# Two chained cross-attentions in float32: heads moved to ACT, a longer lead of the query products, an earlier turned weight, and the last subtile placed among the output products

## The chip, the core and the metric

The kernel runs on one core of one Trainium2 chip. The metric is the device time of one execution in microseconds (us); the median of three runs before the change is 1940.47 us. The engines are called PE (TensorE, with PEld for its weight loads), DVE (VectorE), ACT (ScalarE), POOL (GpSimd) and SP (SyncE, which here only issues DMA transfers). ACT and POOL issue DMA transfers too.

## The reference

There are B=4 sequences of L=1024 tokens with width H=1024, all float32, and a context of S=64 tokens per sequence. Two cross-attention layers follow each other.

```python
# layer 0: 32 query heads of 32, 8 key/value heads
q = x @ Wq + bq;  k = ctx @ Wk + bk;  v = ctx @ Wv + bv
scores = q k^T / sqrt(32) + mask[b, 1, L, S]
out = (softmax(scores) @ v) @ Wo + bo
x = layernorm(out + x) * gamma + beta
# layer 1: 16 heads of 64
a = layernorm(ctx) * ln_gamma + ln_beta
Q = x @ Wq1^T;  K = a @ Wk1^T;  V = a @ Wv1^T
scores = Q K^T / 8, masked keys set to -inf
x = x + tanh(gate) * (softmax(scores) @ V) @ Wo1^T
```

## The kernel before

**Tiles.** The 4096 tokens are 32 subtiles of 128, four blocks of 8 subtiles (`SUB`, `NBLK`; a block is one sequence), or 16 pairs of subtiles. Large products use a seven-product scheme in the manner of Strassen: of a weight and of the token block, quarters and sums of quarters are kept (`B11`, `T1`, `S2`, `N4` and so on), and seven products of half size give what eight would.

**Layer-0 queries.** `query_steps` (L559) is a list of 28 products for a block. Each is four matmul instructions with 512 columns (the trace counts eight) into one of four single PSUM banks (`wx`). `keep` (L576) lets ACT copy a bank to SBUF with the bias, `add` (L582) lets DVE add another bank to that copy, and `put` (L579) stores the result to `qTd` in DRAM over SP's queue. `load_queries` (L636) fetches a subtile's queries from there. The four copies per block are named e, z, u and f; e, u and f share three buffers, z has two.

**Layer-0 attention.** `mix(t, count)` works on subtile t and calls, between its steps, `count` items of a generator `other_work`. The steps of a subtile have two halves of 16 heads: `front` (scores, L669, and mask add, L673), `largest` (maximum, L680, and its subtraction, L683), exponentials on ACT, `total` (sum, L700, reciprocal, L701), `divide` (L704). Of a subtile up to 18 (`by_turning`), the 16 heads of half 0 are exponentiated on ACT one by one (`some`, L687), with the negative maximum as bias and the sum accumulated, so that L683 and L700 are left out for them. The other half is one ACT instruction (`others`, L695). The probabilities are turned through DRAM for these subtiles: `p` is stored (L717) and read back as quarters `pq` (L721), both on POOL's queue, and DVE turns blocks of 32x32 (`turn_quarters`, L405). From subtile 19 on, PE transposes them (`turn`, L396) and ACT copies them (L400). Then come `values` (L740), a copy `oT` by ACT (L389) and its store `oTd` on ACT's queue (L746). The tile `s` of a subtile has two buffers, two-bank PSUM tiles (`big`) are two.

**The other work.** `other_work` (L906) gives the query products of blocks 1 to 3 and then, for each of 8 chunks k of the layer-1 query weight wq1, the folding of the layer-1 keys into that weight (`folded_queries`, L836): one item in which PE turns the chunk (L396) and ACT copies it (L387), and four items `heads` (L850, copied by ACT at L856); the results `a` are stored to `ad` (L862). Within it the quarters of w_o are loaded at the start, their four sums (L181 to L184) are made after chunk 3, and the first pair's tiles `o` and `r` are loaded after chunk 5. `AHEAD = 4` items run before subtile 0; the other 80 are spread evenly over subtiles 0 to 23; eight fold items follow, and the other 32 over subtiles 24 to 31. So the first queries of a block are loaded after the last of its 28 products.

**After attention.** The last subtile (31) is turned and multiplied, the pools of attention are closed, new ones are opened, and `left_out` makes the four differences of the first pair. Then a loop over 16 pairs does the output products (`project`, L421: seven products, L429, gathered by DVE, L437) with a list `fill` of small steps between them: `folded_values` (L877, L882) for the first 8 pairs, and the layer norm of the pair before. Layer 1 follows with the same kind of products on the folded weights.

**Order.** The program is traced in the order of the Python code, and a scheduler then reorders instructions on each engine by estimated costs, with DMA issues on the queue of the engine that issues them. `keep_in_program_order` pins an instruction behind all that were traced before it on its engine. Engines start instructions in that order. Semaphores join the engines.

**The first block.** Before attention starts, the loop over `query_steps(0, ...)` runs the first 28 products; a dictionary `fills` gives the steps after which the next block's rows are turned by DVE. Ahead of this the layer-0 keys and values are stored to `kTd` and `vTd` (L814).

Of the kernel before, what the change touches and what calls it, by code (L numbers as in the profile page):

```python
# [14 lines left out]
P = 128  # L15
H = 1024
# [18 lines left out]
BY_HEAD = 16  # L35
# [36 lines left out]
def tile_two_cross_attentions(  # L72
# [56 lines left out]
    bd = dram.tile([B, H, H], F32, tag="bd", name="bd")  # L129

# [55 lines left out]

    def right_weight(w, tag, name, turned=False):

        r = {"B11": block_of(w, 0, 0, tag, f"{name}_B11", turned)}
        r["T1"] = block_of(w, 0, 1, tag, f"{name}_B12", turned)  # L190
        r["B22"] = block_of(w, 1, 1, tag, f"{name}_B22", turned)
        r["B21"] = block_of(w, 1, 0, tag, f"{name}_B21", turned)
        for n in ("T3", "T2", "N4"):
            r[n] = new_block(tag, f"{name}_{n}")
        return r, right_sums(r)
# [195 lines left out]
    def turn(nat, dst, singles=False):  # L391

        ps = [wx(), wx()] if singles else big()
        for k in range(KC):
            at = ps[k // HK][:, sub_ap(k % HK)] if singles else ps[:, sub_ap(k)]
            nc.tensor.transpose(at, nat[:, sub_ap(k)], ident)  # L396
        if singles:
            copy_out(dst.rearrange("p k l -> p (k l)"), ps)
        else:
            nc.scalar.copy(dst, ps.rearrange("p (k l) -> p k l", k=KC))  # L400

    def turn_quarters(t, dst, ks):

        k0, k1 = ks
        nc.vector.transpose(  # L405
            dst.rearrange("p k (u i) -> p k u i", i=Q),
            t[:, :, k0 * Q : k1 * Q].rearrange("p u (k j) -> p k u j", j=Q),
        )
# [234 lines left out]
    def attend0(t):  # L643
# [12 lines left out]

        n = BY_HEAD if by_turning(t) else 0

# [20 lines left out]
        def largest(e):  # L679
            nc.vector.tensor_reduce(mx[:, e], heads[:, e], AX.XY, ALU.max, negate=True)  # L680
            k = slice(0 if e else n, 16)
# [15 lines left out]
        def total(e):  # L697
            k = slice(0 if e else n, 16)
# [7 lines left out]
        exps = [lambda lo=lo: some(lo, min(lo + 4, n)) for lo in range(0, n, 4)]  # L706
        exps = exps[:1] + [lambda: others(1)] + exps[1:] if n else [lambda: others(0), lambda: others(1)]
# [114 lines left out]

    early_cm.close()
# [12 lines left out]
    def folded_queries(kT, wch, k):  # L836

        wT = wpool.tile([P, KC, P], F32, tag="wb", name=f"wq1T_{k}")
        st = [wpool.tile([P, B, 512], F32, tag="wb", name=f"a_{k}_{n}") for n in range(2)]

        def first():
            turn(wch, wT, True)
# [23 lines left out]
        return [first] + [lambda cc=cc: heads(cc) for cc in range(4)]  # L866
# [26 lines left out]
    def load_outputs(pair):  # L893
        o = (o2pool if pair else early).tile([P, KC, 2 * P], F32, tag="o2", name=f"o2_{pair}")
        nc.sync.dma_start(out=o, in_=oTd[pair])
        r = []
        for u in range(2):
# [3 lines left out]
            nc.sync.dma_start(out=ru, in_=x[sub_ap(t), :])  # L901
# [4 lines left out]
    def other_work(rows):  # L906
# [20 lines left out]
        wch = chunk(wq1, 0, "wq1")  # L927
        w_o, w_o_sums = right_weight(wo0, "wa", "wo0", "heads")
        bo_sb = constant(bo0.partition_broadcast(P), [P, H], "bo", F32, fold)
        for k in range(KC):  # L930
            ahead = chunk(wq1, k + 1, "wq1") if k + 1 < KC else None
            for step in folded_queries(kT, wch, k):
                step()
                yield
            wch = ahead
            if k == 3:
                run(w_o_sums)
            if k == 5:
                first_outputs = load_outputs(0)
# [4 lines left out]
    AHEAD = 4  # L944
# [269 lines left out]
```

## Time and profile before

| | us |
|---|---|
| runs | 1940.96, 1937.8, 1940.47 |
| median | 1940.47 |
| the profiled execution's own time | 1938.62 |
| its span, from first to last instruction | 1936.8 |
| PE busy | 1880.2 |
| DVE busy | 1307.3 |
| ACT busy | 384.6 |
| front of subtile 0 starts | 193.84 |
| front of subtile 20 starts | 529.30 |
| front of subtile 24 starts | 605.23 |
| last subtile's transposes start | 714.59 |

A sum of changes is made against 1938.62; what lies outside its span is 1.82 us, and the median is 1.85 us above it. The last four rows are read from the timeline of PE; they cut the kernel into the stages that the text below speaks of. "Busy" counts an engine's instructions without DMA issues and waits; an instruction's row in the groups has its mean duration in nanoseconds, and the idle time ahead of it with what ended most of it. A wait "X <- Y" in the list of waits names the instruction that waited and the one that released it; the numbers are total us, times, longest us. The row PEclk, and the granted clock in a window, are TensorE's clock as a share of full speed.

### The profile page before, as it was taken

How to read it: one execution, taken by the hardware profiler on the slowest of the kernel's cores; microseconds unless marked ns; L12 is line 12 of the kernel's file. 1: busy time of each engine (PE TensorE's matmuls, PEld its weight loads, DVE VectorE, ACT ScalarE, POOL GpSimd, SP SyncE). 2: the span in 40 equal slices, each digit the busy share in tenths (PEclk: the TensorE clock that was granted, in tenths of full speed). 3: DMA queues.
4: the chain of work that ended last, by engine and by line, in shares of the span. 5: the costliest groups of instructions: out<-in, count | busy, mean ns of one | idle time of the engine just before them, and what ended most of it. 6: DMA issues, size and time to landing. Idle time of an engine off the chain costs nothing.

```text
span 1936.8 us, 17075 instructions
## 1 busy us (share of the span) xinstructions
PE 1880.2 (97%) x6160; PEld 890.1 (46%) x6160; DVE 1307.3 (67%) x1572; ACT 384.6 (20%) x1028; POOL 135.8 (7%) x134
## 2 busy tenths in 40 slices
PE   8999999998998889999999999999999999999999
PEld 7744444444445654334344444444444444444444
DVE  3424799898878974566478777557665766576653
ACT  1111554553435761221200001000000000000000
POOL 0000111111100102111122200000000000000000
PEclk9999999999999889999999999999999999999999
DMA  8971689797768875666673344374747474747421
GB/s 281 184 187 65 171 243 269 231 258 232 232 184 249 266 257 184 218 208 191 215 208 119 130 110 122 99 180 125 179 127 177 128 176 130 174 131 173 120 87 43
DMA packets 218180, 342.10 MB, mean 177 GB/s; under 512 B 25456, under 2 KB 140528, under 8 KB 213104
## 3 DMA queue, kind: packets, MB, share of 16 engines
q1 hardware_dynamic: 156736, 255.03, 46.8%
q10 hardware_dynamic: 52544, 46.14, 8.6%
q0 software_dynamic: 8816, 39.85, 7.1%
q8 instruction: 48, 0.79, 0.2%
q14 instruction: 36, 0.29, 0.1%
HBM read 203.34 MB, written 137.63 MB: 176 GB/s over the span
## 4 chain that ended last, share of the span: by engine, by line
PE 80%; DVE 12%; DMA 3%; issue 3%; ACT 2%; POOL 0%; SPq 0%; DVEq 0%; ACTq 0%; POOLq 0%
PE wx L429 58%; PE wx L565 12%; PE big L669 2%; DVE mx L680 2%; DVE s L673 2%; PE wx L368 1%; PE big L368 1%; PE big L877 1%; DVE s L683 1%; DVE pT L405 1%; DMA q<-qTd 1%; DVE sm L700 1%; DVE s L704 1%; PE big L740 1%; ACT s L687 1%
## 5 line engine op out<-in xcount | busy, mean ns | idle before, releaser
L437 DVE TENSOR_TENSOR r<-wx,r 128x512 f32<-128x512 f32 x224 | 153.5, 686 | 236.3 <-PE wx L429 223.4
L491 ACT ACTIVATE s<-s 128x1024 f32<-128x1024 f32 x32 | 33.7, 1057 | 651.8 <-DVE s L490 651.8
L441 DVE TENSOR_TENSOR s<-wx,key_bias 128x512 f32<-128x512 f32 x64 | 44.1, 690 | 136.7 <-PE wx L429 136.7
L565 PE MATMUL wx<-xT,wq_S 128*128 128x512 f32 x256 | 119.0, 600 | 0.8 <-ACT z L576 0.8
L429 PE MATMUL wx<-wo_B,S 128*128 128x512 f32 x256 | 117.1, 600 | 1.9 <-DVE r L437 1.9
L902 POOL TENSOR_TENSOR r<-r,bo 128x1024 f32<-128x1024 f32 x32 | 82.1, 2571 | 491.9 <-DMA r<-in_x_dram 184.0
L429 PE MATMUL wx<-b_B,pT 128*128 128x512 f32 x256 | 115.8, 593 | 0.6 <-ACT pT L400 0.6
L565 PE MATMUL wx<-xB,wq_A 128*128 128x512 f32 x256 | 116.1, 598 | 0.0
L429 PE MATMUL wx<-b_B,S_p 128*128 128x512 f32 x256 | 116.0, 596 | 0.0
L429 PE MATMUL wx<-a_B,xT 128*128 128x512 f32 x256 | 115.4, 592 | 0.0
L429 PE MATMUL wx<-a_B,S_x 128*128 128x512 f32 x256 | 115.3, 593 | 0.1
L429 PE MATMUL wx<-wo_B,o 128*128 128x512 f32 x256 | 114.6, 595 | 0.0
L687 ACT ACTIVATE s<-s,mx 128x64 f32<-128x64 f32 x304 | 101.1, 335 | 55.4 <-DVE mx L680 49.3
L673 DVE TENSOR_TENSOR s<-big,m 128x1024 f32<-128x1024 f32 x64 | 77.2, 1219 | 38.2 <-PE big L669 38.1
L669 PE MATMUL big<-kv,q 64*128 64x128 f32 x1024 | 86.3, 301 | 9.5 <-DMA q<-qTd 9.3
L669 PEld LDWEIGHTS big<-kv,q 64*128 64x128 f32 x1024 | 74.6, 204 | 43.7 <-issue 36.7
L405 DVE STREAM_TRANSPOSE pT<-pq 128x1024 f32<-128x1024 f32 x66 | 77.9, 1219 | 1.8 <-DMA pq<-p 1.8
L429 PEld LDWEIGHTS wx<-wo_B,S 128*128 128x128 f32 x256 | 47.1, 190 | 68.6 <-issue 51.2
L704 DVE TENSOR_TENSOR s<-s,sm 128x1024 f32<-128x1024 f32 x64 | 76.8, 1219 | 0.9
L429 PEld LDWEIGHTS wx<-wo_B,o 128*128 128x128 f32 x256 | 48.0, 190 | 63.5 <-issue 61.9
L429 PEld LDWEIGHTS wx<-a_B,S_x 128*128 128x128 f32 x256 | 48.5, 190 | 62.0 <-issue 58.3
L429 PEld LDWEIGHTS wx<-a_B,xT 128*128 128x128 f32 x256 | 48.7, 190 | 61.2 <-issue 60.5
(158 smaller groups left out, 2916.4 us busy)
## 6 DMA issues: line engine op xcount, KB each, us to landing
p<-s POOLq DMA_DIRECT2D x19, 1024.0 KB, 7.6
pq<-p POOLq DMA_DIRECT2D x76, 256.0 KB, 5.8
xq<-in_x_dram SPq DMA_DIRECT2D x64, 256.0 KB, 10.0
q<-qTd SPq DMA_DIRECT2D x32, 512.0 KB, 7.6
oTd<-oT ACTq DMA_DIRECT2D x32, 512.0 KB, 6.8
ad<-a SPq DMA_DIRECT2D x16, 1024.0 KB, 6.4
o<-oTd SPq DMA_DIRECT2D x16, 1024.0 KB, 5.3
r<-in_x_dram SPq DMA_DIRECT2D x32, 512.0 KB, 5.5
```

The lines of the kernel that those rows point to most:

```text
L368: nc.tensor.matmul(ps[:, 0:256], w[k // HK, c // HK][:, k % HK, sub_ap(c % HK)], ct[:, k, :], start=(k == 0), stop=(k == KC - 1),)
L405: nc.vector.transpose(dst.rearrange("p k (u i) -> p k u i", i=Q), t[:, :, k0 * Q : k1 * Q].rearrange("p u (k j) -> p k u j", j=Q),)
L429: nc.tensor.matmul(bank, a[s][:, k, :], w[m][:, k, :], start=first and k == 0, stop=last and k == HK - 1, skip_group_check=True,)
L437: nc.vector.tensor_tensor(at, bank, at, ALU.add)
L441: nc.vector.tensor_tensor(at, bank.rearrange("p (h s) -> p h s", s=S), bias.unsqueeze(1).to_broadcast([P, 512 // S, S]), ALU.add,)
L565: nc.tensor.matmul(bank, w_q[a][:, k, sub_ap(i)], rows[b][:, k, :], start=first and k == 0, stop=last and k == HK - 1, skip_group_check=True,)
L669: nc.tensor.matmul(ps[:, at : at + P], q[on, c * 4 + g, :], k0bd[on, b, c, :], start=True, stop=True,)
L673: nc.vector.tensor_tensor(quarters[:, :, c * 8 : (c + 1) * 8], ps.rearrange("p (k a l) -> p a k l", a=NQ, l=Q), mask.rearrange("p e (h l) ...
L680: nc.vector.tensor_reduce(mx[:, e], heads[:, e], AX.XY, ALU.max, negate=True)
L687: nc.scalar.activation(heads[:, 0, k], heads[:, 0, k], AF.Exp, bias=mx[:, 0, k : k + 1], accum_out=sm[:, 0, k : k + 1],)
L704: nc.vector.tensor_tensor(heads[:, e], heads[:, e], wide(sm[:, e]), ALU.mult)
L902: nc.gpsimd.tensor_tensor(ru, ru, bo_sb, ALU.add)
```

## The change

1. `BY_HEAD` becomes a pair (16, 8): of half 1 too, eight heads of subtiles 0 to 18 are exponentiated one by one on ACT, 24 in all; L683 and L700 of that half cover eight heads in place of 16.
2. The layer-1 query weight is turned in the first block. A pool of two buffers of rows and two of columns takes each chunk of 128 rows with four loads on SP's queue; DVE turns it (`turn_quarters`, pinned in program order) after steps 6, 8, 10, 12, 14, 16, 19 and 21; four stores on POOL's queue write it to `wq1T` in DRAM. The folding later loads `turned_chunk(k)` from there. An item of PE transposes per chunk is gone, so that 32 fold items are left of 40.
3. `AHEAD` becomes 6. Blocks 1 and 2 are spread as 28 products over 8 subtiles each, so that the lead is still 6 when the next block begins; over subtiles 16 to 23 come the other 22. `FOLD_AHEAD = 6` fold items follow, and 26 over subtiles 24 to 31.
4. The loads of the quarters of w_o come after chunks 1 to 4 and their sums after chunk 5. `left_out` of the first pair is moved into `other_work`, its result in the pool `early`, and the first pair's loads are pinned.
5. The turning of subtile 31, its values, the closing and opening of pools and the loads of the second pair become the first entries of `fill`, between the first pair's output products.

```diff
@@ -32,7 +32,7 @@
 QW = H // NQ
 PPB = NPAIR // B
 HEADS0 = 32
-BY_HEAD = 16
+BY_HEAD = 16, 8
 
 
 
@@ -127,6 +127,7 @@
     vTd = dram.tile([P, KC, B * S], F32, tag="vTd", name="vTd")
     ad = dram.tile([B, H, H], F32, tag="ad", name="ad")
     bd = dram.tile([B, H, H], F32, tag="bd", name="bd")
+    wq1T = dram.tile([H, H], F32, tag="wq1T", name="wq1T")
 
     def open_pool(stack, name, bufs, side="left"):
         return stack.enter_context(tc.tile_pool(name=name, bufs=bufs, side=side, reuse_waits="tile"))
@@ -184,14 +185,23 @@
             lambda: tt(r["N4"], r["B21"], r["T2"], ALU.subtract),
         ]
 
+    def right_loads(w, tag, name, turned=False):
+
+        r = {}
+
+        def load(n, i, j):
+            r[n] = block_of(w, i, j, tag, f"{name}_B{i + 1}{j + 1}", turned)
+
+        def last():
+            load("B21", 1, 0)
+            for n in ("T3", "T2", "N4"):
+                r[n] = new_block(tag, f"{name}_{n}")
+
+        return r, [lambda: load("B11", 0, 0), lambda: load("T1", 0, 1), lambda: load("B22", 1, 1), last]
+
     def right_weight(w, tag, name, turned=False):
-
-        r = {"B11": block_of(w, 0, 0, tag, f"{name}_B11", turned)}
-        r["T1"] = block_of(w, 0, 1, tag, f"{name}_B12", turned)
-        r["B22"] = block_of(w, 1, 1, tag, f"{name}_B22", turned)
-        r["B21"] = block_of(w, 1, 0, tag, f"{name}_B21", turned)
-        for n in ("T3", "T2", "N4"):
-            r[n] = new_block(tag, f"{name}_{n}")
+        r, loads = right_loads(w, tag, name, turned)
+        run(loads)
         return r, right_sums(r)
 
     def run(steps):
...
@@ -654,7 +660,7 @@
         mx = small.tile([P, 2, 16], F32, tag="mx0", name=f"mx_0_{t}")
         sm = small.tile([P, 2, 16], F32, tag="sm0", name=f"sm_0_{t}")
 
-        n = BY_HEAD if by_turning(t) else 0
+        alone = BY_HEAD if by_turning(t) else (0, 0)
 
         def wide(v):
             return v.unsqueeze(2).unsqueeze(3).to_broadcast([P, v.shape[-1], 2, Q])
@@ -678,24 +684,24 @@
 
         def largest(e):
             nc.vector.tensor_reduce(mx[:, e], heads[:, e], AX.XY, ALU.max, negate=True)
-            k = slice(0 if e else n, 16)
+            k = slice(alone[e], 16)
             if k.start < 16:
                 nc.vector.tensor_tensor(heads[:, e, k], heads[:, e, k], wide(mx[:, e, k]), ALU.add)
 
-        def some(lo, hi):
+        def some(e, lo, hi):
             for k in range(lo, hi):
                 nc.scalar.activation(
-                    heads[:, 0, k], heads[:, 0, k], AF.Exp, bias=mx[:, 0, k : k + 1],
-                    accum_out=sm[:, 0, k : k + 1],
+                    heads[:, e, k], heads[:, e, k], AF.Exp, bias=mx[:, e, k : k + 1],
+                    accum_out=sm[:, e, k : k + 1],
                 )
 
         def others(e):
-            k = slice(0 if e else n, 16)
+            k = slice(alone[e], 16)
             if k.start < 16:
                 nc.scalar.activation(heads[:, e, k], heads[:, e, k], AF.Exp)
 
         def total(e):
-            k = slice(0 if e else n, 16)
+            k = slice(alone[e], 16)
             if k.start < 16:
                 nc.vector.tensor_reduce(sm[:, e, k], heads[:, e, k], AX.XY, ALU.add)
             nc.vector.reciprocal(sm[:, e], sm[:, e])
@@ -703,8 +709,13 @@
         def divide(e):
             nc.vector.tensor_tensor(heads[:, e], heads[:, e], wide(sm[:, e]), ALU.mult)
 
-        exps = [lambda lo=lo: some(lo, min(lo + 4, n)) for lo in range(0, n, 4)]
-        exps = exps[:1] + [lambda: others(1)] + exps[1:] if n else [lambda: others(0), lambda: others(1)]
+        if by_turning(t):
+            one_by_one = [
+                [lambda e=e, lo=lo: some(e, lo, lo + 4) for lo in range(0, alone[e], 4)] for e in range(2)
+            ]
+            exps = one_by_one[0][:1] + [lambda: others(1)] + one_by_one[1] + one_by_one[0][1:]
+        else:
+            exps = [lambda: others(0), lambda: others(1)]
         return front, largest, exps, total, divide
 
     def outputs0(t):
@@ -813,13 +824,36 @@
     for dst, kvT in kv1:
         nc.sync.dma_start(out=dst, in_=kvT)
     kv1_cm.close()
+    wq1_cm = ExitStack()
+    wq1pool = open_pool(wq1_cm, "wq1", 2, "right")
+
+    wq1_rows = {}
+
+    def load_wq1(n):
+        if n < KC:
+            wq1_rows[n] = wq1pool.tile([P, NQ, QW], F32, tag="rows", name=f"wq1_{n}")
+            load_quarters(wq1_rows[n], wq1[sub_ap(n), :])
+
+    def turn_wq1(n):
+
+        cols = wq1pool.tile([P, KC, P], F32, tag="cols", name=f"wq1c_{n}")
+        tc.keep_in_program_order(turn_quarters(wq1_rows.pop(n), cols, (0, KC)))
+        load_wq1(n + 2)
+        to = wq1T[:, sub_ap(n)].rearrange("(a k j) i -> a j k i", a=NQ, j=Q)
+        for a in range(NQ):
+            nc.gpsimd.dma_start(out=to[a], in_=cols[a * Q : (a + 1) * Q])
+
+    for n in range(2):
+        load_wq1(n)
     steps = query_steps(0, rows)
     rows, fills = rows0(1)
+    fills.update({n: lambda i=i: turn_wq1(i) for i, n in enumerate((6, 8, 10, 12, 14, 16, 19, 21))})
     for n, step in enumerate(steps):
         step()
         if n in fills:
             fills[n]()
 
+    wq1_cm.close()
     early_cm.close()
     qpool = open_pool(attention, "q0", 2, "right")
     spool = open_pool(attention, "scores", 2, "right")
@@ -833,13 +867,14 @@
         nc.sync.dma_start(out=t, in_=w[sub_ap(k), :])
         return t
 
-    def folded_queries(kT, wch, k):
-
-        wT = wpool.tile([P, KC, P], F32, tag="wb", name=f"wq1T_{k}")
+    def turned_chunk(k):
+        t = wpool.tile([P, KC, P], F32, tag="wb", name=f"wq1T_{k}")
+        nc.sync.dma_start(out=t, in_=wq1T[:, sub_ap(k)].rearrange("(c p) i -> p c i", p=P))
+        return t
+
+    def folded_queries(kT, wT, k):
+
         st = [wpool.tile([P, B, 512], F32, tag="wb", name=f"a_{k}_{n}") for n in range(2)]
-
-        def first():
-            turn(wch, wT, True)
 
         def heads(cc):
             banks = [wx(), wx()]
@@ -863,7 +898,7 @@
                     out=ad[:, sub_ap(k), n * 512 : (n + 1) * 512].rearrange("b p o -> p b o"), in_=st[n]
                 )
 
-        return [first] + [lambda cc=cc: heads(cc) for cc in range(4)]
+        return [lambda cc=cc: heads(cc) for cc in range(4)]
 
     def folded_values(vT, wch, c):
 
@@ -892,13 +927,17 @@
 
     def load_outputs(pair):
         o = (o2pool if pair else early).tile([P, KC, 2 * P], F32, tag="o2", name=f"o2_{pair}")
-        nc.sync.dma_start(out=o, in_=oTd[pair])
+        load = nc.sync.dma_start(out=o, in_=oTd[pair])
+        if not pair:
+            tc.keep_in_program_order(load)
         r = []
         for u in range(2):
             t = pair * 2 + u
             ru = (rpool.tile([P, H], F32, tag="r", name=f"r_{t}") if pair
                   else early.tile([P, H], F32, tag="r", name=f"r_{t}", bufs=2))
-            nc.sync.dma_start(out=ru, in_=x[sub_ap(t), :])
+            load = nc.sync.dma_start(out=ru, in_=x[sub_ap(t), :])
+            if not pair:
+                tc.keep_in_program_order(load)
             nc.gpsimd.tensor_tensor(ru, ru, bo_sb, ALU.add)
             r.append(ru)
         return o, r
@@ -924,57 +963,60 @@
         early = open_pool(early_cm, "early", 1)
         kT = fold.tile([P, KC, B * S], F32, tag="kvT", name="kT")
         nc.sync.dma_start(out=kT, in_=kTd)
-        wch = chunk(wq1, 0, "wq1")
-        w_o, w_o_sums = right_weight(wo0, "wa", "wo0", "heads")
+        wT = turned_chunk(0)
+        w_o, w_o_loads = right_loads(wo0, "wa", "wo0", "heads")
         bo_sb = constant(bo0.partition_broadcast(P), [P, H], "bo", F32, fold)
         for k in range(KC):
-            ahead = chunk(wq1, k + 1, "wq1") if k + 1 < KC else None
-            for step in folded_queries(kT, wch, k):
+            ahead = turned_chunk(k + 1) if k + 1 < KC else None
+            for step in folded_queries(kT, wT, k):
                 step()
                 yield
-            wch = ahead
-            if k == 3:
-                run(w_o_sums)
+            wT = ahead
+            if k in (1, 2, 3, 4):
+                w_o_loads[k - 1]()
             if k == 5:
-                first_outputs = load_outputs(0)
+                run(right_sums(w_o))
+                o, r = load_outputs(0)
+
+        first_outputs = left_out(o, early, "0_0"), r
 
     fold_cm, early_cm = ExitStack(), ExitStack()
     fold = early = bo_sb = w_o = first_outputs = None
     work = other_work(rows)
-    AHEAD = 4
+
+
+    AHEAD, FOLD_AHEAD = 6, 6
 
     def go_on(n):
         for _ in range(n):
             next(work)
 
-    n = 28 * (NBLK - 1) - AHEAD
     go_on(AHEAD)
     last = NSUB - SUB
     for t in range(last):
-        mix(t, (t + 1) * n // last - t * n // last)
-    go_on(2 * AHEAD)
-    n = 5 * KC - 2 * AHEAD
+        n = 28 - AHEAD if t // SUB == NBLK - 2 else 28
+        mix(t, (t % SUB + 1) * n // SUB - t % SUB * n // SUB)
+    go_on(FOLD_AHEAD)
+    n = 4 * KC - FOLD_AHEAD
     for i in range(SUB):
         mix(last + i, (i + 1) * n // SUB - i * n // SUB)
     next(work, None)
-    flip, values = turned.pop(NSUB - 1)
-    for c in range(2):
-        flip(c)
-    values()
-    attention.close()
-
-
-    last_cm = ExitStack()
-    inner = ExitStack()
-    lpool = open_pool(inner, "left", 1, "right")
-    o2pool = open_pool(inner, "o2", 2, "right")
-    stage = ExitStack()
-    rpool = open_pool(stage, "res", 6, "right")
-    c2 = open_pool(stage, "const2", 1, "right")
-    gamma0_sb, beta0_sb = (
-        constant(ap.partition_broadcast(P), [P, H], n, F32, c2)
-        for ap, n in ((gamma0, "gamma0"), (beta0, "beta0"))
-    )
+
+    last_cm, inner, stage = ExitStack(), ExitStack(), ExitStack()
+    lpool = o2pool = rpool = gamma0_sb = beta0_sb = None
+
+    def open_stage():
+        nonlocal lpool, o2pool, rpool, gamma0_sb, beta0_sb
+        attention.close()
+        lpool = open_pool(inner, "left", 1, "right")
+        o2pool = open_pool(inner, "o2", 2, "right")
+        rpool = open_pool(stage, "res", 6, "right")
+        c2 = open_pool(stage, "const2", 1, "right")
+        gamma0_sb, beta0_sb = (
+            constant(ap.partition_broadcast(P), [P, H], n, F32, c2)
+            for ap, n in ((gamma0, "gamma0"), (beta0, "beta0"))
+        )
+
     vT = fold.tile([P, KC, B * S], F32, tag="kvT", name="vT")
     nc.sync.dma_start(out=vT, in_=vTd)
 
@@ -1008,13 +1050,20 @@
 
         return [lambda: half(0), lambda: half(1), blocks]
 
-    fill = []
-    ahead_o, ahead_r = first_outputs
-    ahead_a = left_out(ahead_o, lpool, "0_0")
+    ahead_a, ahead_r = first_outputs
     wch = chunk(wo1, 0, "wo1")
+
+    def load_second():
+        nonlocal ahead_o, ahead_r
+        ahead_o, ahead_r = load_outputs(1)
+
+
+    ahead_o = None
+    flip, values = turned.pop(NSUB - 1)
+    fill = [lambda: (flip(0), flip(1)), lambda: (values(), open_stage()), load_second]
     for pair in range(NPAIR):
         r, a = ahead_r, ahead_a
-        if pair + 1 < NPAIR:
+        if 0 < pair < NPAIR - 1:
             ahead_o, ahead_r = load_outputs(pair + 1)
         if pair < KC:
             ahead_w = chunk(wo1, pair + 1, "wo1") if pair + 1 < KC else None
```

More of the change, by code (lines that the diff above doesn't have):

```diff
@@ L389, in copy_out, with turn @@
             nc.scalar.copy(dst, ps)
-    def turn(nat, dst, singles=False):
-        ps = [wx(), wx()] if singles else big()
+    def turn(nat, dst):
+        ps = big()
         for k in range(KC):
[L395 to L400, printed above, removed]
+            nc.tensor.transpose(ps[:, sub_ap(k)], nat[:, sub_ap(k)], ident)
+        nc.scalar.copy(dst, ps.rearrange("p (k l) -> p k l", k=KC))
     def turn_quarters(t, dst, ks):
         k0, k1 = ks
-        nc.vector.transpose(
+        return nc.vector.transpose(
             dst.rearrange("p k (u i) -> p k u i", i=Q),
```

## Prediction

> **What bounds the kernel now.** I read the busy row and the slices of the page, then the waits, then windows cut at the starts of the fronts of subtiles 0, 20 and 24, then the chain and the PE timeline where a wait stood out.
>
> ```profile
> PE 1880.2 (97%) x6160; PEld 890.1 (46%) x6160; DVE 1307.3 (67%) x1572; ACT 384.6 (20%) x1028; POOL 135.8 (7%) x134
> PE   8999999998998889999999999999999999999999
> DVE  3424799898878974566478777557665766576653
> ACT  1111554553435761221200001000000000000000
> DMA  8971689797768875666673344374747474747421
> ```
>
> PE is busy 97% of the span; the little room lies in slices 5 to 15 (48 us each), where DVE and ACT are at their fullest: layer-0 attention. What comes after is products of a full PE. So the change can win only where PE runs below 9, or where it takes work off PE.
>
> ```profile
> 193.84:529.30 335.46, 323.35 (x1485) 147.90 (x1484) 291.44 (x292) 165.99 (x687) 50.79 (x93) 0.99 0.81 233
> 529.30:605.23 75.93, 69.20 (x410) 36.45 (x407) 61.17 (x59) 32.09 (x44) 1.37 (x3) 0.99 0.67 182
> 605.23:714.54 109.31, 90.69 (x784) 69.34 (x784) 98.67 (x96) 75.20 (x116) 5.84 (x2) 0.89 0.86 269
> ```
>
> Columns: window, length, busy PE, PEld, DVE, ACT, POOL, granted clock, DMA share, GB/s. Stage A (subtiles 0 to 19) is PE's with DVE close behind (87%) and DMA at 0.81; PE's idle time is 12.1 us. Stage C (subtiles 24 to 31) is DVE's: 98.7 of 109.3 us, with PE idle 18.6 us and its clock down to 0.89.
>
> ```profile
> PE big L669 <- DMA q<-qTd: 9.3, 3, 4.9
> PE big L740 <- DVE pT L405: 6.3, 7, 2.2
> ```
> ```profile
> 328.45 2.06 PE L669 MATMUL big<-kv,q 64*128 64x128 f32 x32 [0.79 <-DMA q<-qTd]
> ```
> ```profile
> 466.70 3.69 PE L669 MATMUL big<-kv,q 64*128 64x128 f32 x32 [4.86 <-DMA q<-qTd]
> ```
> ```profile
> 605.23 3.78 PE L669 MATMUL big<-kv,q 64*128 64x128 f32 x32 [3.67 <-DMA q<-qTd]
> ```
> ```profile
> 594.67 2.20 DVE wo_T L182
> 596.87 0.61 DVE z L582
> 597.50 2.01 DMA qTd<-z
> 599.56 5.62 DMA q<-qTd
> 605.23 0.79 PE big L669 x3
> ```
>
> The three waits for queries are the first fronts of blocks 1 to 3: the query goes out and comes back through DRAM (2.01 + 5.62 us here; 5.90 + 5.23 at the second) after the last product's add. A front after a stop takes 3.7 us where the one at 328.45 takes 2.06: the granted clock is 0.54 in 466.70 to 470.40. At the third, the w_o sum at 594.67 sits ahead of that add on DVE.
>
> ```profile
> 714.59 3.67 PE L396 MATMUL big<-ident,s 128*128 128x128 f32 x16 [2.19 <-DVE s L704]
> 718.20 2.23 PE L740 MATMUL wx<-pT,kv 64*32 64x512 f32 x16
> 720.36 3.70 PE L429 MATMUL wx<-wo_B,o 128*128 128x512 f32 x8
> ```
>
> The last subtile ends alone: PE waits for its division, then transposes and values run cold, and only then the first output product.
>
> **The change, part by part.** Durations are those rows'; sums are against the profiled execution, 1938.62 us, 1.85 under the median of the runs.
>
> *First block.* Two more products before the first front: 2 x 3.5 = +7.0 us here, given back in A. The turning of wq1 enters: 32 loads on SP, 8 DVE transposes of 1.22 us, 32 stores on POOL. DVE has cover (19.25 of 50 us busy in 150 to 200), DMA too (0.19). SP has less: it issues in order, and the loads of chunks 0 to 2 stand ahead of the puts of f_0 and z_0. The store of kTd takes 10.7 us from its issue at 112.84; chunk 0 waits for it, and chunk 2 for the transpose of chunk 0. With a quarter load at 10.0 us (row of xq) and an issue of 0.33 us each, I put that put at about 135 instead of 127.4. ACT reuses that buffer for f_1, which it keeps at 135.25; PE then stalls 0 to 1.5 us, and later rounds fit (one chunk per two products, 7 us). The transposes are pinned in program order on DVE: a late chunk holds the adds z_1, e_3 and those behind them, then their puts, then ACT's keeps of the next use. POOL has nothing else to do before subtile 0's p store. +1 us; bounds 0 and 8 (every one of eight links late by 1).
>
> *Stage A.* (1) Six products of lead at blocks 1 and 2: 6 x 3.5 = 21 us cover the way through DRAM (11 us at its slowest). Gone are 0.79 + 4.86 us of waits and about 2 us of cold front: -7.7. (2) Products between fronts 0 and 20 rise from 69.25 to 70.75 by the order of PE's instructions, +1.5 x 3.5 = +5.3. With the first block's +7.0 the balance is repaid behind subtile 20 (7.25 instead of 10.75 products: -12.3). (3) Eight more heads of 19 subtiles go one by one on ACT. L683 and L700 for that half shrink by half: 2 x 0.61 x 19 = -23 us of DVE. ACT pays 8 x 0.335 less half of one 1.05 us batch = +2.15 per subtile, +41 us: from 166 to 207 of 330, 63%. Neither sets the end while PE does. What PE feels is DVE arriving sooner: of 6.3 us waiting for pT, and about 6 us of second halves running late behind it, I take half, -6. Bounds: 0 and -12. The order of ACT's instructions puts 20 heads in a row (6.7 us) ahead of some copies of values; with four single banks a product's keep can wait 10 us without stopping PE.
> A dense PE would need some 70.75 x 3.5 + 40 half-fronts x 1.09 + 17 values x 1.15 = 311 us; forecast 335.5 + 5.3 - 7.7 - 6 = 327, which keeps 16 us of switching and waits. I do not take those: they are not named by any wait.
>
> *Rule against row.* The row gives 0.335 us a head (x304, 101.1 us): 27 took 4.54 us, so pairs do not overlap further. The Trainium skill (ScalarE: Activation LUTs, What ACT_TABLE_LOAD costs) has an ACTIVATE with a pointer bias at 280 ns + 0.833 ns per element, neighbours overlapping by some 93 ns: an estimate of 240 ns for 64 elements. By the rule ACT pays 8 x 0.240 - 0.53 = 1.4 a subtile, +26 us; by the row +41. The heads here also read an accumulator (188 ns). Row taken; the forecast holds for both, the slower rival only for the row.
>
> *Stages B and C.* Together 529.30 to 714.59 = 185 us, mostly DVE's. The products behind subtile 20 fall by 3.5 (-12.3 us of PE). The first wait (3.67 us for PE, 5.48 for DVE) loses its cause: the w_o sums come earlier, in part, and q_24 is followed by 14.6 us of DVE work on its side before its first add. PE loses the 64 transposes of wq1 (8 x 1.04 = -8.4 us), ACT 16 copies of 0.593 (-9.5), yet DVE bounds here and neither counts directly. DVE's need: 12 subtiles x 11.95 (five pairs at 2.35, two reciprocals at 0.1) + sums 9.2 + subtraction for the first pair 2.8 + adds 2.5 = 158; idle before was 185 - 160 = 25, of which the DVE wait for q_24 is 5.5, waits behind the turning and its clock some 9. I leave 10: 168 us, -17. Of that -12.3 is the repayment above, -5 is gain. Bounds: 163 (half the idle) and 176.
> The added loads of wq1T (512 KB a chunk, as before, in 512-byte rows) stand on SP beside a DMA share of 0.86; they are asked for a chunk ahead, about 8 us. Their nearest row is the load of qTd, same size and rows: 7.6 us. Nothing, at most +4. The first pair's loads of o and x are pinned on SP behind the store of ad of chunk 5; they are wanted a subtile (13 us) later by DVE's subtraction, and 5.3 us is the row of o<-oTd: nothing; if the store of ad is late, the loads of wq1T queue behind them, then the heads on PE, which is idle enough there.
>
> *Rule against row, the clock.* C's clock is 0.89 with no PE gap above 2.2 us but the first. The skill (TensorE: Matmul & The Clock Gate, What's actually happening) says the clock halves only after a window of about 3.4 us idle. By the rule, less PE work in C leaves it warm: 9.5 us a subtile. By the row more idle means more cold: 9.5/0.87 = 10.9. Both lie under DVE's 12.3, so the sum stays; a wholly cold PE (19) would cost C 50 us, but it would then have no idle time to be cold for.
>
> *The end of layer 0.* The first output product starts before the last division; transposes and values come between products. 714.59 to 720.36 was exposed: 5.8 us, of which warm transposes and values keep 3.2 on PE and the wait of 2.19 and the cold goes: -4.8; the first product runs ahead in time that was idle. The reordered folded values and SP loads are hidden behind 3.5 us products: 0. The rest of the kernel is unchanged: 0.
>
> *Sum.* +1 (first block) + 7.0 lead, - 8.4 (A: 335.5 to 327), - 17 (B and C), - 4.8 = -22 us. 1938.6 - 22 = 1916.4, and +1.85 for the median: 1918.
>
> **The rivals.**
> *A smaller gain: the way through DRAM sets stage A.* Probabilities go out (7.6 us) and back (5.8), at a DMA share of 0.81; a wait of 11.26 us for p<-s stands on the chain at 496.79. If PE's pT waits come from DMA, freeing DVE brings nothing, and the idle time of C stays too. Left: 7.7 + 4.8 + the q_24 wait of 3 - 1 - 5 (not recovered) = 6 to 12, 1929 to 1935. Against it: DVE waited for pq only 1.8 us in all. Chance 0.20.
> *No change*: the lead costs what it saves, and ACT's longer chain takes the rest; within 0.2% (3.9 us, about what can be told from no change). 0.06.
> *Slower: ACT's queue in stage A.* A subtile's heads last 8.6 us on ACT in place of 6.4; division 0, p's store and the copy of values that frees one of two double banks come up to 2.2 us later. ACT waits already show `ACT s L687 <- DVE mx L680: 49.3`: DVE's maximum comes late, ACT then works in a burst. If PE's front waits for that copy, the whole 2.2 x 19 = 42 us land on PE; less the 22, the time is about 1960. It decides from 22/19 = 1.2 us a subtile on. Against it: PE waits for no copy of values in the trace of before, a subtile takes 16.8 us and ACT 10.4 of it. Here too I count part of the SP ring in the first block: eight chunks through two buffers; at loads of 25 us instead of 10 it alone costs 25 us. 0.16.
>
> **How the numbers follow.** Forecast 0.58 (own range 1907 to 1927), smaller gain 0.20, no change 0.06, slower 0.16. The range 1906 to 1938 leaves out the slower case and a few hundredths on either side. Faster 0.78, same 0.06, slower 0.16.
>
> **What would show it.** Right: the first front near 202; no wait of a front for q<-qTd above 1 us at subtiles 8, 16 and 24; the window from front 0 to front 20 near 327 with ACT over 200 us busy and DVE near 268; L396 without wq as source; the first output product ahead of the last transposes, near 697. Wrong: PE waiting for oT's or a keep's ACT row, or for s L704, over 1 us a subtile; f or z keeps waiting for qTd stores before 194; C still at 109 us with DVE waiting for big L669.

## The result: 10 us faster, where 22 were forecast

| us | before | changed |
|---|---|---|
| median of the runs | 1940.72 | 1930.22 (1928.65 to 1932.89) |
| the profiled execution | 1938.62 | 1932.89 |
| front of subtile 0 starts | 193.84 | 205.72 |
| front 0 to front 20 (stage A) | 335.4 | 335.2 |
| front 20 to front 24 (B) | 76.0 | 60.8 |
| front 24 to the last product of the first pair | 140.3 | 136.8 |
| from there to the end of the span | 1191.3 | 1192.6 |

The ratio to the kernel before is 0.9953 (95% interval 0.9939 to 0.9966). The changed kernel's profiled execution is the slowest of its four runs, so the stages add up to 5.7 us and not to the 10.5 of the medians. Rows of stages below are read from profiled executions, gains from medians. The forecast of 1918 and its range up to 1938 took the right direction and twice the size.

The page of the changed kernel, the same rows as before:

```profile
PE 1870.2 (97%) x6096; PEld 877.7 (45%) x6096; DVE 1299.0 (67%) x1580; ACT 418.6 (22%) x1316; POOL 154.9 (8%) x166
PE   8999998999998889999999999999999999999999
DVE  3425488689889974566578777557665766576653
ACT  1101465656635652121100001000000000000000
```

Ten us of PE work are gone, most of it the transposes of wq1, and ACT has 34 us more. The windows from front 0 to 20, 20 to 24, and 24 to about the end of attention (columns as before):

```profile
205.72:540.88 335.16, 326.07 (x1495) 148.18 (x1494) 274.92 (x292) 208.88 (x992) 50.60 (x93) 0.99 0.84 238
540.88:601.71 60.83, 55.50 (x350) 29.23 (x346) 53.60 (x51) 23.64 (x30) 1.43 (x3) 0.97 0.67 181
601.71:703.00 101.29, 80.11 (x719) 59.53 (x720) 97.45 (x99) 67.72 (x105) 6.23 (x2) 0.92 0.90 280
```

In stage A, ACT rose from 166.0 to 208.9 us as forecast, and DVE fell from 291.4 to 274.9 (to 268 by the forecast), yet the stage is as long as before. It holds one and a half products more, as forecast (567 matmuls of L571 in place of 555, eight to a product), which is 5.3 us. The waits of PE in the changed kernel tell the rest. The first two lines are its fronts' and values' waits; the third is in the first block:

```profile
PE big L675 <- DMA q<-qTd: 0.4, 1, 0.4
PE big L751 <- DVE pT L411: 7.4, 6, 5.2
PE wx L571 <- DVE u L588: 2.9, 1, 2.9
```

The waits for queries are gone (9.3 before), those for the turned probabilities are not (6.3 before). One of them alone is 5.2 us, and the values behind it run at a granted clock of 0.50: they take 2.96 us, against 2.10 behind each of the five shorter waits (0.2 to 1.1 us). PE's timeline around it:

```profile
328.35 2.74 PE L571 MATMUL wx<-xT,wq_A 128*128 128x512 f32 x6
336.28 2.96 PE L751 MATMUL big<-pT,kv 64*32 64x512 f32 x16 [5.19 <-DVE pT L411]
339.17 2.07 PE L571 MATMUL wx<-xT,wq_A 128*128 128x512 f32 x2
341.18 1.26 PE L675 MATMUL big<-kv,q 64*128 64x128 f32 x16
```

Front 8, at 341.18, has its queries in time, but PE stood still 5 us earlier for something else.

### The profile page after: what moved, and what is told of

It is laid out like the page before. It is cut to its first block, busy times and chain, and to the rows that moved or that the text cites. A ratio compares the mean times of both kernels' runs of the same rounds, so it can differ in the third digit from the quotient of the medians.

```text
span 1931.1 us, 17386 instructions
## 1 busy us (share of the span) xinstructions
PE 1870.2 (97%) x6096; PEld 877.7 (45%) x6096; DVE 1299.0 (67%) x1580; ACT 418.6 (22%) x1316; POOL 154.9 (8%) x166
## 4 chain that ended last, share of the span: by engine, by line
PE 81%; DVE 10%; DMA 4%; ACT 3%; issue 2%; SPq 0%; POOL 0%; ACTq 0%; DVEq 0%
PE wx L435 58%; PE wx L571 14%; PE big L675 2%; DVE s L679 2%; PE wx L378 1%; PE big L378 1%; DVE mx L686 1%; PE big L912 1%; PE big L751 1%; DMA oTd<-oT 1%; ACT s L693 1%; DVE s L689 1%; DVE sm L706 1%; DVE s L710 1%; DMA o<-oTd 1%
## 5 line engine op out<-in xcount | busy, mean ns | idle before, releaser
L693 ACT ACTIVATE s<-s,mx 128x64 f32<-128x64 f32 x456 | 151.8, 336 | 63.2 <-DVE mx L686 54.7
L571 PE MATMUL wx<-xT,wq_S 128*128 128x512 f32 x256 | 116.7, 597 | 1.6 <-ACT z L582 1.6
L571 PE MATMUL wx<-xB,wq_A 128*128 128x512 f32 x256 | 116.0, 598 | 0.0
L675 PEld LDWEIGHTS big<-kv,q 64*128 64x128 f32 x1024 | 70.3, 193 | 43.6 <-issue 37.5
L693 ACT ACTIVATION_READ_ACCUMULATOR s<-s,mx 128x1 f32 x456 | 85.9, 188 | 0.0
L675 PE MATMUL big<-kv,q 64*128 64x128 f32 x1024 | 81.6, 290 | 1.2 <-DVE s L679 0.5
```

What stands on the lines that cost most here:

```text
L571: nc.tensor.matmul(bank, w_q[a][:, k, sub_ap(i)], rows[b][:, k, :], start=first and k == 0, stop=last and k == HK - 1, skip_group_check=True,)
L675: nc.tensor.matmul(ps[:, at : at + P], q[on, c * 4 + g, :], k0bd[on, b, c, :], start=True, stop=True,)
L693: nc.scalar.activation(heads[:, e, k], heads[:, e, k], AF.Exp, bias=mx[:, e, k : k + 1], accum_out=sm[:, e, k : k + 1],)
```

## Experiments

Where nothing else is said, a kernel is the changed one with the edit shown. The kernels ran in three groups, each with the kernel before beside them: its median was 1939.55 in the first two (the first eight kernels) and 1940.88 in the third (the last four). Ratios are to that median, with their 95% intervals in brackets; the changed kernel's is 0.9939 to 0.9966. Where two such intervals overlap, the difference of two kernels is not clear of noise.

**One part undone at a time.**

```diff
-BY_HEAD = 16, 8
+BY_HEAD = 16, 0
```


> Against the changed kernel, with only its first part undone (16 heads on ACT in place of 24). Theory P: from subtile 0 to 20 the kernel is held by the way of the probabilities through DRAM (store 8.8 us, load 6.1 us, two buffers of scores), not by DVE's busy time, so the 23 us of DVE work that come back change little: within 3 us of the changed kernel (1930), the first front at 205.7, front 0 to front 20 in 333 to 338 us. Theory Q (ACT's queue): the 8 heads delay the division and the store of p, so taking them off ACT makes the kernel faster by 5 us or more. Theory D (DVE as the prediction had it): slower by 6 us or more.

1934.26, ratio 0.9976 (0.9965 to 0.9988): 4 us slower than the changed kernel (the intervals just touch, but the fastest run of the one, 1933.20, is slower than the slowest of the other, 1932.89), so the heads on ACT gain, and more work in ACT's queue does not cost time. From front 0 to front 24 its trace has 400.8 us in place of 396.0. The result lies between Theory P and Theory D and decides neither.

```diff
-    AHEAD, FOLD_AHEAD = 6, 6
+    AHEAD, FOLD_AHEAD = 4, 6
...
-        n = 28 - AHEAD if t // SUB == NBLK - 2 else 28
-        mix(t, (t % SUB + 1) * n // SUB - t % SUB * n // SUB)
+        n = 28 * (NBLK - 1) - AHEAD
+        mix(t, (t + 1) * n // last - t * n // last)
```


> The changed kernel with four products of lead, spread evenly over 24 subtiles as before. Theory P: the waits of fronts 8 and 16 for their queries come back (5 to 6 us of PE idle time) but the wait of 5.2 us for pT near 331 goes, because PE comes to it later: slower by 1 to 4 us. Theory D: the whole 7.7 us come back, slower by 7 or more. Fronts start 7 us earlier at subtile 0 in both.

1923.99, ratio 0.9922 (0.9909 to 0.9936): 6 us faster, against both theories. The waits of fronts 8 and 16 came to 0 and 1.31 us (0.79 and 4.86 before) and that of front 24 to 2.19 (3.67), although the lead was as short as before.

The third kernel turns wq1 on PE in the folding again: the loads, turns and stores of the first block are taken out, and an item of eight transposes and two copies (`first`) stands ahead of each chunk's four.

```diff
-    fills.update({n: lambda i=i: turn_wq1(i) for i, n in enumerate((6, 8, 10, 12, 14, 16, 19, 21))})
...
-        return [lambda cc=cc: heads(cc) for cc in range(4)]
+        return [first] + [lambda cc=cc: heads(cc) for cc in range(4)]
...
-            ahead = turned_chunk(k + 1) if k + 1 < KC else None
+            ahead = chunk(wq1, k + 1, "wq1") if k + 1 < KC else None
...
-    AHEAD, FOLD_AHEAD = 6, 6
+    AHEAD, FOLD_AHEAD = 6, 8
...
-    n = 4 * KC - FOLD_AHEAD
+    n = 5 * KC - FOLD_AHEAD
```


> The changed kernel with wq1 turned by PE in the folding again and nothing of it in the first block. Theory P: the first front comes 4 to 5 us earlier (no add of u behind turns of wq1 on DVE, no cold product), and the stage from front 24 to the second pair's first product is longer by 2 to 5 us, because DVE bounds it and PE's 8.4 us lie mostly in its idle time: between 3 us faster and 2 us slower in all. If PE counts there in full, slower by 4 us.

1930.14, ratio 0.9953 (0.9938 to 0.9968): no difference. Front 0 came at 200.90, 4.8 us earlier, and front 24 to the first pair's last product took 142.6 us, 5.8 longer. What this part gains in the folding, it pays in the first block.

```diff
-    fill = [lambda: (flip(0), flip(1)), lambda: (values(), open_stage()), load_second]
+    flip(0)
+    flip(1)
+    values()
+    open_stage()
+    fill = [load_second]
```


> The changed kernel with subtile 31 turned and multiplied ahead of the first output product, as before. If this part is worth what the prediction gave it: slower by 4 to 5 us. If the first product of the pair only waits for the copy of the values of subtile 30 on ACT (it started at 708.9, cold, 3.3 us before the last division ended): slower by 2 to 3 us.

1935.73, ratio 0.9979 (0.9968 to 0.9990): 5.5 us slower. This part is worth about what the prediction gave it (4.8).

**One part alone on the kernel before.** If a lead of four hides the queries, something else must have. The first kernel is the one before with only the heads' part of the diff, in `attend0`:

```diff
-BY_HEAD = 16
+BY_HEAD = 16, 8
...
-            k = slice(0 if e else n, 16)
+            k = slice(alone[e], 16)
```


> The kernel before with the first part alone: 24 heads on ACT. Theory R (new, after lead 4 came out 6 us faster than the changed kernel): DVE's relief brings the query adds forward, so that most of the waits of fronts 8 and 16 for their queries go without any longer lead: front 0 to front 20 falls from 335.4 to 328 us or less, the kernel is 5 to 9 us faster than before. If DVE's relief only helps together with other parts: within 3 us of before.

1927.37, ratio 0.9933 (0.9920 to 0.9946): 12 us faster, as much as the whole change by itself (1927.37 against 1930.22; the intervals overlap). Its groups of DVE and PE from front 0 to front 20:

```profile
L683 DVE TENSOR_TENSOR s<-s,mx 128x512 f32<-128x512 f32 x19 | 13.0, 687 | 0.4
L669 PE MATMUL big<-kv,q 64*128 64x128 f32 x648 | 47.2, 286 | 3.4 <-DMA q<-qTd 2.2 <-ACT oT L389 0.7
L745 PE MATMUL big<-pT,kv 64*32 64x512 f32 x288 | 30.9, 600 | 3.8 <-DVE pT L405 2.6 <-issue 1.1
```

With DVE relieved, PE waits 2.2 us for queries here (9.3 with front 24 before, now 2.6) and 2.6 for pT, though the lead is the old one. Stage A takes 330.96 us, 4.5 less than before, with one product more in it (563 matmuls in place of 555); from front 20 to the first pair's last product it is 211.9 in place of 216.2 us, with one product less.

```diff
-    AHEAD = 4
+    AHEAD = 6
...
-        mix(t, (t + 1) * n // last - t * n // last)
-    go_on(2 * AHEAD)
-    n = 5 * KC - 2 * AHEAD
+        n = 28 - AHEAD if t // SUB == NBLK - 2 else 28
+        mix(t, (t % SUB + 1) * n // SUB - t % SUB * n // SUB)
+    go_on(8)
+    n = 5 * KC - 8
```


> The kernel before with the third part alone: six products of lead, 28 a block. Theory R: the waits for queries go (9.3 us of PE), but the two more products in the first block cost 7 us there and come back only in part, and the wait for pT grows: between 3 us faster and 4 us slower than before. Theory D (the prediction's account): faster by 5 us or more.

1937.50, ratio 0.9988 (0.9979 to 0.9996): 2 us faster, only just clear of noise. PE's waits in it:

```profile
PE big L740 <- DVE pT L405: 9.5, 6, 4.4
PE big L669 <- DMA q<-qTd: 0.4, 1, 0.4
```

The lead alone took away 8.9 us of waiting for queries, but the wait for pT grew by 3.2 us, and front 0 came 7.0 us later. So each part alone removes most of the same 9.3 us: the heads 6.7, the lead 8.9.

**The lead, apart from the spread.**

```diff
-    AHEAD, FOLD_AHEAD = 6, 6
+    AHEAD, FOLD_AHEAD = 4, 6
```


> The changed kernel with a lead of four products, but 28 products a block as in the change. It tells the lead from the spread. If the two products in the first block are what costs: as fast as the kernel with four products spread evenly (1924), with front 0 at 198.4. If the spread (70.75 in place of 69.25 products between fronts 0 and 20) costs: 1928 to 1931.

1923.45, ratio 0.9911 (0.9898 to 0.9924): 6.8 us faster than with a lead of six, as much as with the even spread (the intervals of the two overlap). So it is the longer lead that costs, not 28 products a block. Windows of this kernel from front 0 to front 20, and on to the first pair's last product; then the same of the changed kernel:

```profile
197.99:526.49 328.50, 321.83 (x1487) 146.30 (x1486) 272.70 (x292) 209.01 (x991) 50.63 (x93) 0.99 0.84 240
526.49:730.07 203.58, 178.39 (x1223) 106.36 (x1219) 166.63 (x169) 108.80 (x157) 14.12 (x8) 0.94 0.83 253
```
```profile
205.72:540.88 335.16, 326.07 (x1495) 148.18 (x1494) 274.92 (x292) 208.88 (x992) 50.60 (x93) 0.99 0.84 238
540.88:738.50 197.62, 168.89 (x1199) 103.47 (x1195) 166.19 (x167) 106.98 (x155) 14.58 (x8) 0.94 0.83 255
```

PE did 9.5 us less behind front 20 with the lead of six (168.89 against 178.39), but the stage became only 6.0 us shorter: DVE has the same 166 us there in both. Ahead of it the lead of six is 7.7 us later at front 0 and 6.7 us longer in stage A (one product more by PE's order, 3.5 us, and more waiting). 14.4 us were paid, 6.0 came back. With a lead of four front 8, at 330.63, does not wait for its queries:

```profile
330.63 1.16 PE L675 MATMUL big<-kv,q 64*128 64x128 f32 x16
```

For the fourth part the loads of w_o go back to the start of the folding and its sums behind chunk 3:

```diff
-            if k in (1, 2, 3, 4):
-                w_o_loads[k - 1]()
+            if k == 3:
+                run(w_o_sums)
             if k == 5:
-                run(right_sums(w_o))
```


> The changed kernel with the quarters of w_o loaded at the start of the folding and summed after chunk 3, as before. Theory R has no strong claim: the four sums (9.2 us of DVE) stand in a stage that DVE bounds wherever they are, so within 3 us of the changed kernel. If the later place is worth the wait of 5.5 us that DVE had for the front of subtile 24: slower by 4 to 6 us.

1932.21, ratio 0.9956 (0.9944 to 0.9968): no difference from the change. DVE's order fits this: the scheduler puts the four sums at nearly the same places, wherever the code asks for them, at 549.6, 559.5, 600.2 and 607.2 us here and at 557.0, 564.5, 599.7 and 606.7 in the changed kernel.

```diff
-    AHEAD, FOLD_AHEAD = 6, 6
+    AHEAD, FOLD_AHEAD = 2, 6
```


> The changed kernel with a lead of two products, 28 a block. Theory R says that a product made ahead of front 0 costs 3.5 us there and comes back behind subtile 20 only in part, while a shorter lead costs waits of the fronts for their queries. Two products less than in the lead of four: front 0 at 191; if the waits are still hidden the kernel gains 3 us more (1920); if they come back (5 us at fronts 8 and 16, and at 24) it loses what it gained, 1924 to 1930.

1925.22, ratio 0.9920 (0.9907 to 0.9933), not distinct from the lead of four. It says little about a lead of two: the scheduler moved products forward, so that 3.5 stood ahead of front 0 in PE's order, and front 0 came at 197.63. The waits for queries did grow:

```profile
PE big L675 <- DMA q<-qTd: 6.7, 4, 3.3
```

**What the wait for pT is.**

```diff
-            nc.gpsimd.dma_start(out=p0[t], in_=s)
...
         divide(1)
+        store_half(t, 1)
...
         divide(0)
+        store_half(t, 0)
```
(`store_half` stores 1024 of the 2048 columns.)


> The changed kernel (lead of six), with the probabilities stored in two halves of 512 KB, each behind its own division. If the wait of 5.2 us for pT near 331 is the way of p through DRAM (the whole store was issued at 311.8, landed 11.2 us later, and the quarters were loaded only then), it shrinks to under 2 us, front 0 to front 20 falls by 3 us or more. If it is DVE's order (rows of the next block ahead of the division), it stays above 3 us.

1926.61, ratio 0.9930 (0.9917 to 0.9943): 3.6 us faster, though the intervals overlap a little. The two signs of the expectation disagree. The wait stayed above 3 us, which speaks for DVE's order:

```profile
333.57 2.97 PE L750 MATMUL big<-pT,kv 64*32 64x512 f32 x16 [4.11 <-DVE pT L411]
```

Stage A fell by 8 us, to 327.1, which was to speak for the way through DRAM. But it holds 14 matmuls of the products less (553 in place of 567), and these come behind front 20: from front 0 to front 24 it is 396.6 us, and 396.0 in the changed kernel. What the trace gains lies behind front 24.

The traces show why the wait hardly moved. The first line is the division that the store of p waits for in the changed kernel, the second the same with the halves:

```profile
310.03 1.22 DVE L710 TENSOR_TENSOR s<-s,sm 128x1024 f32<-128x1024 f32 x1
314.11 1.22 DVE L710 TENSOR_TENSOR s<-s,sm 128x1024 f32<-128x1024 f32 x1
```

From the issue of the last store to the issue of the last loads of quarters it is 11.8 us in the changed kernel (311.81 to 323.60) and 7.7 with the halves (315.89 to 323.55). So the halves did shorten the way through DRAM by 4.1 us, and DVE, which now had other work ahead of the division, came to it 4.1 us later. In both kernels DVE does sums of the next block's rows ahead of this division (303.24 to 310.1 in the changed one). Order and way lie one behind the other on this chain; which of them the wait is owed to was not taken apart.

**The wait in the first block.** DVE's timeline in the changed kernel, and PE's:

```profile
159.78 2.37 DVE L411 STREAM_TRANSPOSE xT<-xq 128x1024 f32<-128x1024 f32 x2 [8.31 <-PE wx L571]
162.07 1.20 DVE L411 STREAM_TRANSPOSE wq1c<-wq 128x1024 f32<-128x1024 f32 x1
163.20 2.25 DVE L182 TENSOR_TENSOR xT<-xT,xB 128x2048 f32<-128x2048 f32 x1
165.37 2.36 DVE L411 STREAM_TRANSPOSE xB<-xq 128x1024 f32<-128x1024 f32 x2
167.65 1.20 DVE L411 STREAM_TRANSPOSE wq1c<-wq 128x1024 f32<-128x1024 f32 x1
168.78 0.65 DVE L588 TENSOR_TENSOR u<-wx,u 128x512 f32<-128x512 f32 x1
```
```profile
169.49 5.40 PE L571 MATMUL wx<-xN,wq_A 128*128 128x512 f32 x8 [2.88 <-DVE u L588]
```

DVE works without a gap from 159.78, two turns of wq1 stand ahead of the add, and PE waits for it to reuse the bank. The wait of 2.88 us and the product behind it, 5.40 us at a granted clock of 0.68 where such products take 3.6 to 3.7, make 4.6 of the 4.9 us by which front 0 is later than the lead alone explains. With the lead of four the same wait is there, but not the slow product:

```profile
170.33 3.70 PE L571 MATMUL wx<-xN,wq_A 128*128 128x512 f32 x8 [2.88 <-DVE u L588]
```

```diff
-enumerate((6, 8, 10, 12, 14, 16, 19, 21))
+enumerate((6, 8, 10, 12, 20, 21, 22, 24))
```


> A lead of four with 28 a block, and the turns of wq1 in the first block after steps 6, 8, 10, 12, 20, 21, 22, 24, so that chunks 4 and 5 no longer stand ahead of the add u_2 on DVE. If those two turns (2.4 us) caused the wait of 2.88 us and the cold product behind it, front 0 starts 3.5 to 4.7 us earlier (193.5 to 194.5) and the kernel is 3 to 5 us faster than with a lead of four alone (1923.5). If SP or the stores were the cause: front 0 unchanged.

1919.31, ratio 0.9894 (0.9878 to 0.9909): the lowest median of all, 21.6 us below the kernel before. It is 4 us below the lead of four alone, but the two intervals overlap (0.9898 to 0.9924 there), and the two profiled executions are equally long (1923.84 and 1923.83), so a gain from the later turns is likely and not shown. Front 0 came at 196.52, 1.5 us earlier and not 3.5 to 4.7. PE's waits for the add in it:

```profile
167.64 3.70 PE L571 MATMUL wx<-xN,wq_A 128*128 128x512 f32 x8 [0.78 <-DVE u L588]
...
180.01 3.70 PE L571 MATMUL wx<-xN,wq_A 128*128 128x512 f32 x8 [0.76 <-DVE u L588]
```

The 2.88 us became 0.78, and 0.76 came in at the next add, where a turn now waits for a store of wq1T.

The last kernel has the lead of four, the later turns and the halves together:


> A lead of four, the turns later, and p stored by halves: the version that the runs so far point to. Theory R: 1917 to 1921. If the halves do not help with a lead of four (pT waits there are 6.5 us in five places), the same as with the turns later alone.

1929.18, ratio 0.9944 (0.9931 to 0.9957): 10 us slower than without the halves, against the expectation. PE waits for queries again (two fronts, 7.6 us):

```profile
PE big L675 <- DMA q<-qTd: 7.6, 2, 4.7
PE big L750 <- DVE pT L411: 6.0, 6, 3.6
```

With the halves, the lead of six (1926.61) has the lower median, though the intervals overlap; without them, the lead of four is faster. Why the halves delay the queries stays open: the edit also changed what the scheduler puts where (551 matmuls of L571 between fronts 0 and 20, in place of 559), and the two were not taken apart.

## Why the prediction was wrong, by its own steps

| us | forecast | profiled executions |
|---|---|---|
| up to front 0 | +8 | +11.9 |
| stage A | -8.4 | -0.3 |
| front 20 to the first pair's last product | -21.8 | -18.7 |
| the rest | 0 | +1.3 |
| sum | -22.2 | -5.7 |

Half of what is missing lies in stage A. The step that failed there is the one that adds the lead's gain (-7.7) to the heads' gain (-6), as if each removed a wait of its own.

- *Stage A (1) and (3): -13.7 together.* Measured at the forecast number of products: -0.3 - 5.3 = -5.6. Both parts work on the same waits. The heads alone, with the old lead, cut the wait for queries from 9.3 to 2.6 us and that for pT from 6.3 to 2.6. The lead alone cuts the first to 0.4 but raises the second to 9.5. Together they leave 0.4 and 7.4. So the -6 for pT, which was to bring this wait to 3 us, came as 1.1 us more, and of the lead's gain most was there without it. The medians say the same: the heads are worth 12.2 us alone and 4.0 as the last part; the lead, with its spread, 2.0 alone and -6.2 as the last part (-6.8 without the spread). Both differ by about 8 us. So do the starts of front 24, by which all query products are done and the lead's price is paid: 605.23 before, 597.76 with the heads alone, 599.79 with the lead alone, and 599.57 with both where PE still turns wq1 (the third kernel above, which has parts 4 and 5 too). The two gains of 7.5 and 5.4 us make 5.7 together.
- *Stage A (3), DVE's work: -23.* Measured -16.5. The two halved instructions take 0.68 us and not 0.61, so the rows of L683 and L700 fell by 20.3 us; other rows grew a little (the reciprocals by 1.3 us).
- *First block, +1 beside the lead's 7.0.* Measured +4.9: front 0 at 205.72 in place of 201.8. The step that failed is "DVE has cover (19.25 of 50 us busy)". An average hid a burst of 9 us just where an add that PE needs stood last. The step followed SP's order at length and not DVE's. With the turns moved away the wait fell to two of 0.8 us.
- *The lead's products, given back behind subtile 20: -12.3.* Two products of lead more cost 14.4 us up to front 20 and gave 6.0 back behind it, by the pair of windows above. From front 20 to the end of the last division (709.83 + 2.35) it is 171.3 us, where 168 was forecast, so the -17 came as -14. What failed is the balance: products went from a stage in which DVE is busy 166 us with them or without, into one in which PE is busy 97% of the time.
- *wq1 off PE.* The prediction counted nothing directly for it. 5.8 us came in the folding and 4.8 were paid in the first block: no difference in the medians.
- *The last subtile, -4.8.* Right: 5.5 us. Its path was not quite the one told. The first product started at 708.90 and not near 697: it waited 2.23 us for ACT's copy of the values of subtile 30 and took 5.40 us, at a granted clock of 0.68:

```profile
708.90 5.40 PE L435 MATMUL wx<-wo_B,o 128*128 128x512 f32 x8 [2.23 <-ACT oT L397]
714.14 1.91 PE L405 MATMUL big<-ident,s 128*128 128x128 f32 x16
715.88 3.60 PE L435 MATMUL wx<-wo_T,S 128*128 128x512 f32 x8
719.41 1.09 PE L751 MATMUL wx<-pT,kv 64*32 64x512 f32 x16
```

- *ACT's price.* 42.9 us more in stage A: the row's +41 stands, not the +26 of the rule set beside it.
- *The rivals.* The smaller gain has the right time (1929 to 1935) but not the mechanism that it names, for freeing DVE does gain, by itself the most of all parts (12.2 us). The way of p through DRAM does stand in the chain of the longest wait, so this rival keeps a share that was not measured. ACT's queue, the slower rival, is refuted: more heads on ACT are faster with the other parts and without. The clock of stage C, 0.89 before, was 0.92, although PE idled a larger share of it (busy 80.1 of 101.3 us, 90.7 of 109.3 before), so more idle time did not make it colder here.

## What to carry to other kernels

When two edits of a change can each remove the same wait, count it once, to the one that costs the bounding engine nothing, and ask what the other still brings. Work moved ahead of a stage is paid in full where its engine is the bound, and in the stage that it left it comes back only as far as no other engine bounds that stage. Cover is a matter of order: look for the burst on the engine's timeline in which the moved instructions will stand, not at its mean share.

## What the hardware showed unexpectedly

The same wait of 2.88 us in the first block was followed by a product of 5.40 us in the changed kernel and with the lead of two (granted clock 0.68), and of 3.70 us with the lead of four (granted clock 1.00). So in this kernel a stop of 2.9 us may or may not cost the clock, which is 1.7 us beside the wait. What decides between the two was not found.
